# A four-layer graph network on one core: adj stored in the order of its reading, its small pieces loaded through GpSimd's queue, and a row added to x by GpSimd in four places

## The chip, the cores and the metric

The kernel is one program on one core of a Trainium2 chip. It is timed in device microseconds, and lower is better. The engines are named as the profile names them: PE (TensorE; PEld is its weight load), DVE (VectorE), ACT (ScalarE), POOL (GpSimd) and SP (SyncE, which only issues DMAs). All arrays are fp32.

## The reference

There are 16 graphs of 1024 nodes with 256 features. `adj` is 16 x 1024 x 1024, sparse, with a full diagonal. Four layers follow each other, each of the form `x = x + layer(relu(layernorm(x)), adj)`:

```python
# layer 0: attention; W_w, W_b, a_w
h = hidden @ W_w.T + W_b; u = mask * exp(e_i + f_j + a_b); h' = (u / sum(u)) @ h
# layer 1: normalised graph convolution; weight, bias
d = (sum(adj) + 1e-5) ** -0.5; out = d * (adj @ (d * (x @ weight))) + bias
# layer 2: 512-unit gates, node after node: node i reads what the nodes before it have become
x_par = norm_adjT[:, i] @ h; r, z = sigmoid(x W + x_par W'); h[i] = z * x_par + (1 - z) * tanh(...)
# layer 3: neighbour sum, two dense layers with an RMS norm between them
```

Only the order in which `adj` is stored for the device, the queue of some loads and the engine of two additions are at issue here. The values are the same.

## The kernel before

The program runs in three parts. `layers_0_1` takes the graphs one after the other in a software pipeline of 17 turns (`for i in range(B + 1)`). `layer_2` walks through 8 blocks of 128 nodes of all graphs. `layer_3` takes the graphs one by one again.

In `layers_0_1` every engine's order is the order in which the Python code runs (`tc.manual_schedule` holds PE, DVE, ACT, POOL and SP), so one late operand holds all that stands behind it on its engine. One turn i, in PE's order:

- `sums(i, ...)` for layer 0: seven products (L373) of quarters of the transposed adjacency with quarters of the features, in the manner of Strassen. Between the products stand hooks `a0` to `a6`, which hold work for the other engines.
- `weights` (L409 on PE, L412 on DVE: `x = po * scale + x`) for layer 0 of graph i and for layer 1 of graph i-1.
- `sums(i, ...)` for layer 1, with hooks `d0` to `d6`; then `degrees(i + 1)` (L450) for the next graph.

The operands of the products are the "quarters": 512 x 512 pieces of `adjT`, 1 MB each, held in ten buffers `at`. `get` (L289) loads five of them a graph; `plus` (L295) adds one to another with an accumulating DMA in POOL's queue; `drop` hands a buffer back. In hook `a0` of turn i, SP issues the load of x for graph i+1 and of three quarters (`b11`, `t1`, `b22`); `t3` and `b21` follow in `d0` and `d1`.

`plus_row` (L348) adds the row `W_b` to all of x after `degrees`, and the row `bias` in hook `d0`. It is an accumulating DMA of 1 MB in POOL's queue, once each a graph.

Beside this runs `orders`, a generator of small DVE steps which computes in what order layer 2 may take the nodes. `side(us)`, called in the hooks, lets so many microseconds of it run, counted by costs that are written beside each `yield`. Its input are the diagonal 128 x 128 blocks of `adj` in "pieces" `pc` of 4 rows. `fetch` (L102) loads a piece with eight DMAs of 32 KB in SP's queue, two pieces ahead of the one in use, into two buffers; `piece` (L107, DVE) waits for it. Each half of the generator, `places` and the chains in `rest`, reads 32 pieces, so there are 64 pieces and 512 DMAs. Between the halves, POOL loads four index tables (`table`, L182).

From turn 9 on, each turn also carries two "jobs" (`Job`), which prepare layer 2: `load` (ad, ab and h2 by SP), `mask` and `scale` (POOL, on ad and ab), `turn`, `first`, `order`, `base` (PE transposes and products, L522, L534, L546, L548), with stores by POOL.

In `layer_2`, `base_tasks.load` (L843) brings one column block `ab` of one graph's adj, 512 KB, 112 times; POOL masks it (L854) before PE uses it (L876).

The layer norms use `inv_sqrt`: a POOL power (L83, `rs` and `dis`) between two DVE instructions.

Of the kernel before, what the change touches and what calls it, by code (L numbers as in the profile page):

```python
# [16 lines left out]
P = 128  # L17
# [23 lines left out]
def gnn_stack(ctx: ExitStack, tc: tile.TileContext, a: dict, out: bass.AP):  # L41
# [51 lines left out]
    def orders(pool, psum):  # L93
# [3 lines left out]
        pieces = deque()  # L97

        def fetch(j0):
            nz = pool.tile([P, R, P], F32, name="pc", bufs=2)  # L100
            for t in range(NT):
                nc.sync.dma_start(nz[t * B : (t + 1) * B], a["adj"][:, t * P + j0 : t * P + j0 + R, t * P : (t + 1) * P])  # L102
            pieces.append(nz)

        def piece(j0, op, value):
# [12 lines left out]
        def places():  # L118
            nc.vector.memset(bins, TOP)
            nc.vector.tensor_scalar(open_, step[:, :S], -1.0, TOP - 1, op0=ALU.mult, op1=ALU.add)  # L120
            nc.vector.tensor_scalar(below, open_, 1.0, None, op0=ALU.add)
            nc.vector.memset(held, 0.0)
            fetch(0)
            fetch(R)
            yield 9.0
            for j0 in range(0, P, R):
                nz = piece(j0, ALU.is_equal, 2 * TOP)
                for j in range(j0, j0 + R):
                    mine = bins[:, j : j + 1]
# [12 lines left out]

            key = tile_("key")
            nc.vector.scalar_tensor_tensor(key, bins, -256.0, step, op0=ALU.mult, op1=ALU.add)
            for i in range(0, P, R):
                less = pool.tile([P, R, P], F32, name="pc", bufs=2)
                nc.vector.tensor_tensor(less, key[:, None].to_broadcast([P, R, P]),
                                        key[:, i : i + R][:, :, None].to_broadcast([P, R, P]), ALU.is_lt)
                nc.vector.tensor_reduce(pos[:, i : i + R], less, AX.X, ALU.add)
                yield 1.4  # L150
            pt = psum.tile([P, 512], F32, name="pt")
            nc.tensor.transpose(pt[:, :P], pos, ident)
            nc.vector.tensor_copy(place, pt[:, :P])
            yield 0.5
# [105 lines left out]
    def layers_0_1():  # L260
        with ExitStack() as st:
# [24 lines left out]

            def get(b, name, m, n):
                Q[b][name] = quarters.pop(0)
                nc.sync.dma_start(Q[b][name], rows(a["adjT"][b])[:, 4 * m : 4 * m + 4, 512 * n : 512 * n + 512])  # L289

            def drop(b, name):
                quarters.append(Q[b][name])
# [26 lines left out]
            class Moments:  # L319


                def __init__(self, x):
                    self.x = x
                    self.sum, self.ssq, self.neg = (small.tile([P, NT], F32, name=n) for n in ("m_sum", "m_ssq", "m_neg"))

                def first(self, tiles):
                    junk = psum.tile([P, 512], F32, name="pt")[:, :D]
# [16 lines left out]
                for t in tiles:  # L344
                    nc.scalar.activation(h[:, t], x[:, t], AF.Relu, bias=shift[:, t : t + 1], scale=scale[:, t : t + 1])

            def plus_row(x, name):
                nc.gpsimd.dma_start(out=x, in_=vec[name][:, None].to_broadcast([P, NT, D]), accum_op=ALU.add)  # L348

            def combos(h):  # L350

# [64 lines left out]
            def begin_f(b, tiles):  # L416
                m = mean[b]
                if tiles[0] == 0:
                    q[b] = big.tile([P, NT, D], F32, name="q")
                    m.f = small.tile([P, NT], F32, name="f")  # L420
                for t in tiles:
                    nc.scalar.activation(q[b][:, t], x[b][:, t], AF.Relu, bias=m.neg[:, t : t + 1])

# [7 lines left out]
            def end_f(b):  # L431
                m = mean[b]
                g[b] = gs
                nc.scalar.activation(g[b][:, :, 0], m.f, AF.Exp, bias=v[:, D : D + 1])
                m.rg = small.tile([P, NT], F32, name="rg")
                nc.vector.tensor_mul(m.rg, m.rs, g[b][:, :, 0])

            def scaled(b, tiles):
# [26 lines left out]
                return rc, deg  # L465

            def inverse(b, deg):
                zero = small.tile([P, NT], F32, name="zero")
                nc.vector.tensor_scalar(zero, deg, 0.0, None, op0=ALU.is_equal)
                safe = small.tile([P, NT], F32, name="safe")  # L470
                nc.vector.tensor_add(safe, deg, zero)
                nc.vector.reciprocal(safe, safe)
                nc.vector.tensor_scalar(zero, zero, -1.0, 1.0, op0=ALU.mult, op1=ALU.add)
                nc.vector.tensor_mul(dinv[:, b], safe, zero)

            class Job:
# [9 lines left out]
                def load(self):  # L486
                    b = self.b
                    self.ad = ad = self.tile("ad", [P, NT, 2 * P])
                    nc.sync.dma_start(ad[:, 0, P:], a["adjT"][b, :P, :P])
                    nc.sync.dma_start(ad[:, 1:], bass.AP(tensor=a["adjT"].tensor, offset=a["adjT"].offset + b * N * N + P * N,  # L490
                                                         ap=[[N, P], [P * N + P, NT - 1], [1, 2 * P]]))
                    self.ab = self.tile("ab", [P, NT, P])
                    nc.sync.dma_start(self.ab, rows(a["adj"][b])[:, :, :P])
                    if b < 14:
                        h2[b] = big.tile([P, NT, D], F32, name="h2", bufs=2)
                        nc.sync.dma_start(h2[b], rows(he_d[b]))
# [109 lines left out]
            add_halves(0, "t1", "t1", "b11")  # L606
            Q[0]["t2"] = quarters.pop(0)
            add_halves(0, "t2", "t1", "b22")
            plus_row(x[0], "W_b")
            left_of, first, second = combos(q[0])  # L610
            first()
            add_halves(0, "t3", "t3", "b22")
# [8 lines left out]
            for i in range(B + 1):  # L621
# [2 lines left out]
                got = {}  # L624

                def a0():
                    if ahead:
                        if i:
                            load_x(i + 1)
                        for name, mh, nh in (("b11", 0, 0), ("t1", 0, 1), ("b22", 1, 1)):  # L630
                            get(i + 1, name, mh, nh)
                    if run_a:
                        run_a.load()
                    side(1.0)
                def a1():
                    second()
                    add_halves(i, "t4", "t2", "b21")
                def a2_():
                    side(3.4)
                def a3():  # L640
                    side(2.6)
                def a4():
                    got["rc"], got["deg"] = over(i, ds)
                    if run_a:
                        run_a.mask()
                    if ahead:
                        mean[i + 1] = Moments(x[i + 1])
                        mean[i + 1].first(lo)
                    side(1.2)
# [72 lines left out]
                def d0():  # L722
                    if ahead:
                        plus(i + 1, "t1", "b11")
                        get(i + 1, "t3", 0, 1)
                    plus_row(x[i], "bias")
                    if m2:
                        m2.first(all_)
                    side(1.5)
                def d1():  # L730
                    second1()
                    if ahead:
                        get(i + 1, "b21", 1, 0)
                        begin_f(i + 1, all_)
                    side(0.6)
                def d2():
                    if m2:
                        m2.middle()
                        m2.second(all_)
                    if ahead:  # L740
                        add_f(i + 1, lo)
                    side(1.0)
                def d3():
                    if ahead:
                        add_f(i + 1, hi)
                        end_f(i + 1)
                    side(0.5)
# [21 lines left out]
                if ahead:  # L769
                    ds = degrees(i + 1)  # L770
                    plus(i + 1, "t3", "b22")
                    plus_row(x[i + 1], "W_b")
                    Q[i + 1]["t4"] = quarters.pop(0)
                if m2:
                    h2[i - 1] = big.tile([P, NT, D], F32, name="h2", bufs=2)
# [25 lines left out]
    def layer_2(shared, early):  # L801
        with ExitStack() as st:
# [33 lines left out]
            def base_tasks(t, bxt):  # L836
# [3 lines left out]

                def load(b):
                    ab = big.tile([P, NT, P], F32, name="ab")
                    nc.sync.dma_start(ab, rows(a["adj"][b])[:, :, t * P : (t + 1) * P])  # L843
                    hb = shared.tile([P, NT, D], F32, name="hb")
                    if t > 2:
                        nc.sync.dma_start(hb[:, : t - 2], rows(hn_d[b])[:, : t - 2])
# [797 lines left out]
```

## Time and profile before

| | |
|---|---|
| time, median of 3 runs | 4663.49 us (4662.62 to 4669.71) |
| profiled execution, its own time | 4668.5 us |
| profiled execution, span | 4666.8 us |
| granted TensorE clock, mean | 0.967 |
| PE busy | 4265.4 us (91%) |
| DVE busy | 2581.4 us (55%) |
| ACT busy | 1605.6 us (34%) |
| POOL busy | 1510.0 us (32%) |
| layers 0 and 1, 0 to 1540 us: PE, DVE, POOL busy | 1294.1, 930.2, 377.1 us |
| layer 2, 1540 to 3350 us: PE, DVE, POOL busy | 1685.5, 823.9, 570.9 us |
| layer 3, 3350 to 4667 us: PE, DVE, POOL busy | 1285.9, 827.2, 562.0 us |

Busy times of different engines overlap. "Idle before" an instruction is the time in which its engine had nothing to run, and the profile names what ended it. One product of four matmuls shows as eight records. The granted clock is the share of its full clock that TensorE was given in a stretch.

### The profile page before, as it was taken

The page shows a single profiled execution, that of the slowest core. Times are in us where ns is not written, and L with a number is a line of the kernel's source. Part 1 is how long each engine was busy: PE and PEld are TensorE (multiplying, and loading weights), DVE is VectorE, ACT ScalarE, POOL GpSimd, SP SyncE. Part 2 cuts the span into 40 slices and gives each one's busy share as a digit, 9 for nine tenths or more (in the row PEclk, how much of TensorE's full clock was granted, in tenths as well). Part 3 has the DMA queues.
Part 4 walks back from the last instruction along what each step waited for, and adds up shares of the span by engine and source line. Part 5 has one row for each costly group of instructions (what it writes and reads, how often), then busy time and mean ns, then how long its engine had stood idle before and what let it go on. Part 6 is the DMA issues. An engine that isn't in the chain of part 4 may idle for free. (4 is left out here: it accounts for less than half of the span.)

```text
span 4666.8 us, 56009 instructions
## 1 busy us (share of the span) xinstructions
PE 4265.4 (91%) x18967; PEld 2923.9 (63%) x18967; DVE 2581.4 (55%) x6213; ACT 1605.6 (34%) x3861; POOL 1510.0 (32%) x1720
## 2 busy tenths in 40 slices
PE   7898998777788799999999999999899999999998
PEld 3444454434445577878787878787655656565656
DVE  6676875455564344444444444445356767676765
ACT  2453554333342222322232322233333333333332
POOL 1111213321233332333222233333144353535352
PEclk9999999888899899999999999999899999999999
DMA  6576767866676644444544445442142323232310
GB/s 184 157 187 176 179 178 210 204 194 195 190 219 183 204 149 146 145 150 141 158 133 142 133 146 161 157 134 87 38 149 82 108 82 109 82 109 82 109 46 19
DMA packets 584232, 659.72 MB, mean 141 GB/s; under 512 B 49952, under 2 KB 480672, under 8 KB 577696
## 3 DMA queue, kind: packets, MB, share of 16 engines
q1 hardware_dynamic: 515168, 478.12, 32.4%
q0 software_dynamic: 68640, 176.45, 14.9%
q8 instruction: 204, 3.34, 0.3%
q14 instruction: 220, 1.80, 0.1%
HBM read 487.47 MB, written 116.65 MB: 129 GB/s over the span
## 5 line engine op out<-in xcount | busy, mean ns | idle before, releaser
L876 PE MATMUL pf<-hb,ab 128*128 128x256 f32 x1568 | 406.3, 381 | 15.5 <-DMA hb<-hs_d 6.2
L988 PE MATMUL pf<-hs,wx 128*128 128x256 f32 x1536 | 349.5, 382 | 22.8 <-POOL hs L979 21.1
L988 PEld LDWEIGHTS pf<-hs,wx 128*128 128x128 f32 x1536 | 290.9, 191 | 66.6 <-POOL hs L979 22.9
L83 POOL TENSOR_TENSOR rs<-rs_v,mhalf 128x8 f32<-128x8 f32 (+1 forms) x65 | 112.2, 1726 | 647.6 <-DVE rs_v L79 413.1
L876 PEld LDWEIGHTS pf<-hb,ab 128*128 128x128 f32 x1568 | 279.5, 190 | 67.5 <-issue 15.2
L1442 PE MATMUL ph<-bxt,hb 128*128 128x512 f32 x704 | 311.0, 598 | 4.7 <-ACT hb L1426 3.9
L409 PE MATMUL pmm<-w,ag 128*128 128x256 f32 x1024 | 253.9, 404 | 64.3 <-DVE ag L397 36.3
L1471 POOL TENSOR_TENSOR ss<-ss,sq 128x512 f32<-128x512 f32 x224 | 280.4, 1271 | 89.4 <-ACT sq L1469 85.6
L409 PEld LDWEIGHTS pmm<-w,ag 128*128 128x128 f32 x1024 | 201.9, 202 | 117.4 <-DVE x L412 40.1
L1532 PEld LDWEIGHTS po<-w,hh 128*128 128x128 f32 x2048 | 236.3, 193 | 9.5 <-issue 7.2
L1532 PE MATMUL po<-w,hh 128*128 128x128 f32 x2048 | 240.4, 277 | 1.4 <-ACT hh L1515 0.7
L1442 PEld LDWEIGHTS ph<-bxt,hb 128*128 128x128 f32 x704 | 133.2, 192 | 165.8 <-issue 160.1
L1276 POOL DMA_INDIRECT hs_d<-h,table x128 | 128.9, 1007 | 330.2 <-ACTq L1262 162.6
L993 DVE TENSOR_TENSOR gates<-pf,bias 128x512 f32<-128x512 f32 x128 | 88.2, 691 | 237.9 <-PE pf L988 230.4
L1514 DVE TENSOR_TENSOR hh<-hh,po 128x512 f32<-128x512 f32 x256 | 154.5, 680 | 96.7 <-PE po L1511 96.7
L1083 ACT ACTIVATE r<-pr 128x256 f32<-128x256 f32 (+3 forms) x230 | 68.0, 347 | 401.8 <-PE pr L1042 384.5
L1469 ACT ACTIVATE sq<-hh 128x512 f32<-128x512 f32 x224 | 141.2, 630 | 164.6 <-DVE hh L1467 126.1
L1024 PE MATMUL pf<-bd,h 128*128 128x384 f32 (+4 forms) x512 | 185.3, 453 | 4.6 <-ACT bs L863 2.8
L1467 DVE SCALAR_TENSOR_TENSOR hh<-ph,b,u 128x512 f32<-128x512 f32 x192 | 144.1, 751 | 65.3 <-PE ph L1463 55.1
L337 ACT ACTIVATE pt<-x,m_neg 128x256 f32<-128x256 f32 x240 | 114.3, 476 | 188.1 <-DVE m_neg L332 181.8
L1027 DVE TENSOR_TENSOR bxt<-bxt,pf 128x384 f32<-128x384 f32 (+4 forms) x256 | 124.9, 500 | 93.9 <-PE pf L1024 85.8
L1515 ACT ACTIVATE hh<-hh,rw 128x512 f32<-128x512 f32 x256 | 160.2, 710 | 15.7 <-DVE hh L1514 15.7
(350 smaller groups left out, 9165.9 us busy)
## 6 DMA issues: line engine op xcount, KB each, us to landing
at<-in_adjT SPq DMA_DIRECT2D x80, 1024.0 KB
ab<-in_adj SPq DMA_DIRECT2D x127, 512.0 KB
bxt<-in_adjT SPq DMA_DIRECT2D x88, 512.0 KB
at<-at POOLq DMA_DIRECT2D x30, 1024.0 KB, 7.5
at<-in_adjT SPq DMA_DIRECT2D x40, 512.0 KB
x<-W_b_sb POOLq DMA_DIRECT2D x16, 1024.0 KB, 14.7
pc<-in_adj SPq DMA_DIRECT2D x512, 32.0 KB
x<-bias_sb POOLq DMA_DIRECT2D x16, 1024.0 KB, 20.4
```

What stands on the lines that cost most here:

```text
L409: nc.tensor.matmul(po[:, t - t0], ag[:, c, t * P : (t + 1) * P], w[:, c], start=c == 0, stop=c == DC - 1)
L876: nc.tensor.matmul(pb, ab[:, jts[k]], hb[:, jts[k]], start=k == 0, stop=k == len(jts) - 1)
L988: nc.tensor.matmul(pg[:, e], wx[:, c, q * D + e * P : q * D + (e + 1) * P], self.hs[:, c], start=c == 0, stop=c == DC - 1)
L1024: nc.tensor.matmul(pf, h[:, g, c * P : (c + 1) * P], bd[:, g, b0 : b0 + n, S : S + far], start=True, stop=True)
L1276: nc.gpsimd.indirect_dma_start(out=hs_d[t][g][:, :], out_offset=row(1, g, t, s), in_=h[:, g], in_offset=None)
L1442: nc.tensor.matmul(pa, h[b][:, mt, c * P : (c + 1) * P], at[b][n0 // NH][:, mt], start=mt == 0, stop=mt == NT - 1)
L1467: nc.vector.scalar_tensor_tensor(hh[q][:, k], ph, b1[:, k : k + 1], u, op0=ALU.add, op1=ALU.add)
L1469: nc.scalar.activation(sq, hh[q][:, k], AF.Square)
L1471: nc.gpsimd.tensor_tensor(ss[q], ss[q], sq, ALU.add)
L1514: nc.vector.tensor_mul(hh[q][:, k], hh[q][:, k], pr)
L1515: nc.scalar.activation(hh[q][:, k], hh[q][:, k], AF.Silu, scale=rw[:, k : k + 1])
L1532: nc.tensor.matmul(po[:, n], left[:, c, n * P : (n + 1) * P], right[:, c], start=onto is None and n == 0 and c == 0, stop=c == HH - 1, ski ...
```

## The change

Four arrays are made on the host, each in the order in which the kernel reads it: `own` (the diagonal blocks, graph and block along the partitions), `quarters` (each 512 x 512 quarter with 8 KB together for each partition), `near` (the two blocks beside the diagonal that a job needs) and `columns` (each 1024 x 128 column block with 4 KB together for each partition). `adj` itself is no longer passed; `adjT` is, for layer 3.

- `fetch` becomes one DMA of 256 KB in POOL's queue, into three buffers instead of two. Six small tiles (`m_sum`, `f`, `rg`, `zero`, `safe`) go from two buffers to one.
- `get`, `Job.load` and `base_tasks.load` read the new arrays. The two loads of `ad` become one.
- `get` of `b11`, `t1` and `b22` moves from `a0` to `a1`, `a2_` and `a4`, so a job's first load comes ahead of them in SP's queue.
- `plus_row` becomes a POOL addition on two of the eight tiles of x. `W_b` is added after `degrees` and in `a0`, `a1` and `a2_`; `bias` in `d0` to `d3`.

```diff
         def fetch(j0):
-            nz = pool.tile([P, R, P], F32, name="pc", bufs=2)
-            for t in range(NT):
-                nc.sync.dma_start(nz[t * B : (t + 1) * B], a["adj"][:, t * P + j0 : t * P + j0 + R, t * P : (t + 1) * P])
+            nz = pool.tile([P, R, P], F32, name="pc", bufs=3)
+            nc.gpsimd.dma_start(nz, a["own"][:, j0 : j0 + R])
             pieces.append(nz)
...
             def get(b, name, m, n):
                 Q[b][name] = quarters.pop(0)
-                nc.sync.dma_start(Q[b][name], rows(a["adjT"][b])[:, 4 * m : 4 * m + 4, 512 * n : 512 * n + 512])
+                nc.sync.dma_start(Q[b][name], a["quarters"][b, m, n])
...
-            def plus_row(x, name):
-                nc.gpsimd.dma_start(out=x, in_=vec[name][:, None].to_broadcast([P, NT, D]), accum_op=ALU.add)
+            def plus_row(x, name, pair):
+                two = slice(2 * pair, 2 * pair + 2)
+                nc.gpsimd.tensor_tensor(x[:, two], x[:, two], vec[name][:, None].to_broadcast([P, 2, D]), ALU.add)
...
-                    nc.sync.dma_start(ad[:, 0, P:], a["adjT"][b, :P, :P])
-                    nc.sync.dma_start(ad[:, 1:], bass.AP(tensor=a["adjT"].tensor, offset=a["adjT"].offset + b * N * N + P * N,
-                                                         ap=[[N, P], [P * N + P, NT - 1], [1, 2 * P]]))
+                    nc.sync.dma_start(ad, a["near"][b])
                     self.ab = self.tile("ab", [P, NT, P])
-                    nc.sync.dma_start(self.ab, rows(a["adj"][b])[:, :, :P])
+                    nc.sync.dma_start(self.ab, a["columns"][b, 0])
...
                 def a0():
-                    if ahead:
-                        if i:
-                            load_x(i + 1)
-                        for name, mh, nh in (("b11", 0, 0), ("t1", 0, 1), ("b22", 1, 1)):
-                            get(i + 1, name, mh, nh)
+                    if ahead and i:
+                        load_x(i + 1)
                     if run_a:
                         run_a.load()
+                    if i:
+                        plus_row(x[i], "W_b", 1)
                     side(1.0)
                 def a1():
+                    if ahead:
+                        get(i + 1, "b11", 0, 0)
+                    if i:
+                        plus_row(x[i], "W_b", 2)
...
                 def a2_():
+                    if ahead:
+                        get(i + 1, "t1", 0, 1)
+                    if i:
+                        plus_row(x[i], "W_b", 3)
...
                 def a4():
+                    if ahead:
+                        get(i + 1, "b22", 1, 1)
...
                 def d0():
...
-                    plus_row(x[i], "bias")
+                    plus_row(x[i], "bias", 0)
...
                 if ahead:
                     ds = degrees(i + 1)
                     plus(i + 1, "t3", "b22")
-                    plus_row(x[i + 1], "W_b")
+                    plus_row(x[i + 1], "W_b", 0)
...
                 def load(b):
                     ab = big.tile([P, NT, P], F32, name="ab")
-                    nc.sync.dma_start(ab, rows(a["adj"][b])[:, :, t * P : (t + 1) * P])
+                    nc.sync.dma_start(ab, a["columns"][b, t])
```

`plus_row(x[i], "bias", k)` stands in `dk` for k = 1, 2, 3 as well, and before the first turn all four pairs of `W_b` are added to `x[0]` at once.

More of the change, by code (lines that the diff above doesn't have):

```diff
@@ L145, in places @@
             for i in range(0, P, R):
-                less = pool.tile([P, R, P], F32, name="pc", bufs=2)
+                less = pool.tile([P, R, P], F32, name="pc", bufs=3)
                 nc.vector.tensor_tensor(less, key[:, None].to_broadcast([P, R, P]),
@@ L323, in __init__ @@
                     self.x = x
-                    self.sum, self.ssq, self.neg = (small.tile([P, NT], F32, name=n) for n in ("m_sum", "m_ssq", "m_neg"))
+                    self.ssq, self.neg = (small.tile([P, NT], F32, name=n) for n in ("m_ssq", "m_neg"))
+                    self.sum = small.tile([P, NT], F32, name="m_sum", bufs=1)
                 def first(self, tiles):
@@ L419, in begin_f @@
                     q[b] = big.tile([P, NT, D], F32, name="q")
-                    m.f = small.tile([P, NT], F32, name="f")
+                    m.f = small.tile([P, NT], F32, name="f", bufs=1)
                 for t in tiles:
@@ L434, in end_f @@
                 nc.scalar.activation(g[b][:, :, 0], m.f, AF.Exp, bias=v[:, D : D + 1])
-                m.rg = small.tile([P, NT], F32, name="rg")
+                m.rg = small.tile([P, NT], F32, name="rg", bufs=1)
                 nc.vector.tensor_mul(m.rg, m.rs, g[b][:, :, 0])
@@ L467, in inverse @@
             def inverse(b, deg):
-                zero = small.tile([P, NT], F32, name="zero")
+                zero = small.tile([P, NT], F32, name="zero", bufs=1)
                 nc.vector.tensor_scalar(zero, deg, 0.0, None, op0=ALU.is_equal)
-                safe = small.tile([P, NT], F32, name="safe")
+                safe = small.tile([P, NT], F32, name="safe", bufs=1)
                 nc.vector.tensor_add(safe, deg, zero)
@@ L608, in layers_0_1 @@
             add_halves(0, "t2", "t1", "b22")
-            plus_row(x[0], "W_b")
+            for pair in range(4):
+                plus_row(x[0], "W_b", pair)
             left_of, first, second = combos(q[0])
@@ L730, in d1 @@
                 def d1():
+                    plus_row(x[i], "bias", 1)
                     second1()
@@ L736, in d2 @@
                 def d2():
+                    plus_row(x[i], "bias", 2)
                     if m2:
@@ L743, in d3 @@
                 def d3():
+                    plus_row(x[i], "bias", 3)
                     if ahead:
@@ L1606 @@
     adj = i["adj"]
+    adjT = adj.transpose(0, 2, 1)
+    tiles = adj.reshape(B, NT, P, NT, P)
+    near = np.zeros((B, P, NT, 2 * P), np.float32)
+    for t in range(NT):
+        lo = max(t - 1, 0) * P
+        near[:, :, t, 2 * P - ((t + 1) * P - lo) :] = adjT[:, t * P : (t + 1) * P, lo : (t + 1) * P]
     given = {
         "x": i["x"],
-        "adj": adj,
-        "adjT": adj.transpose(0, 2, 1),
+        "adjT": adjT,
+        "own": np.stack([tiles[:, t, :, t] for t in range(NT)]).reshape(NT * B, P, P),
+        "quarters": adjT.reshape(B, 2, 4, P, 2, 512).transpose(0, 1, 4, 3, 2, 5),
+        "near": near,
+        "columns": tiles.transpose(0, 3, 2, 1, 4),
         "W_w": i["L0_gnn_W_w"],
```

## The prediction

> **What bounds the kernel now.** I read the stretches first, one for each turn of the graph loop, cut where PE starts `degrees` (L450). Columns: us, then PE, PEld, DVE, ACT, POOL busy, granted clock, DMA share, GB/s.
>
> ```profile
> 415.80:496.60 80.80, 71.08 (x229) 36.52 (x230) 55.10 (x196) 36.35 (x105) 13.56 (x10) 0.96 0.65 168
> 496.60:564.60 68.00, 67.90 (x225) 35.77 (x224) 55.29 (x121) 36.35 (x105) 13.94 (x10) 1.00 0.72 186
> 638.30:707.00 68.70, 68.46 (x225) 35.70 (x224) 50.77 (x213) 36.34 (x105) 13.57 (x10) 1.00 0.71 184
> ...
> 1036.80:1175.00 138.20, 96.61 (x328) 53.13 (x328) 68.27 (x187) 41.76 (x115) 33.77 (x29) 0.83 0.66 189
> 1301.50:1395.80 94.30, 86.09 (x339) 50.00 (x338) 63.35 (x180) 41.77 (x115) 33.37 (x29) 1.00 0.78 231
> ```
>
> The same work takes PE 68 us without idle time in two turns, and 77 to 81 us in the five turns before them. With two jobs it takes 94.3 us in the last row and 126.4, 138.2 and 126.5 us in the three turns ahead of it. PE is the bound where a turn is short; elsewhere something holds PE, and its clock drops as well. The waits of 0 to 1540 us name it, PE's and then DVE's (us in total, times, longest):
>
> ```profile
> PE pz L373 <- DVE ag L393: 69.3, 7, 16.5
> PE pmm L409 <- DVE ag L397: 36.3, 6, 7.7
> PE pmm L409 <- DVE x L412: 24.5, 9, 8.6
> ```
>
> ```profile
> DVE pc L107 <- DMA pc<-in_adj: 155.2, 21, 17.1
> ```
>
> PE waits for DVE, which has nothing wrong with it but that it stands at a piece. The timelines of PE, DVE and SP show one such place:
>
> ```profile
> 973.79 6.59 PE L373 MATMUL pz<-at,q 128*128 128x512 f32 x8 [15.38 <-DVE ag L393]
> ```
>
> ```profile
> 967.82 0.38 DVE L107 TENSOR_SCALAR pc<-pc 128x416 f32<-128x416 f32 x1 [15.48 <-DMA pc<-in_adj]
> ...
> 973.05 0.68 DVE L393 TENSOR_TENSOR ag<-pz,ag 128x512 f32<-128x512 f32 x1
> ```
>
> ```profile
> 910.58 33.89 SPq L102 DMA_DIRECT2D pc<-in_adj  x24
> 944.64 0.38 SPq L274 DMA_DIRECT2D x<-in_x  x1
> 945.14 2.50 SPq L289 DMA_DIRECT2D at<-in_adjT  x3
> 947.74 1.65 SPq L489 DMA_DIRECT2D ad<-in_adjT  x1
> ```
>
> The pieces for 967 us stand in SP's queue behind the loads of x, three quarters and a job, issued from 944.6 to 958.2 us, and SP itself was held at older pieces until 944.5. The order of one queue is the bound here, not a busy engine. After 1540 us little is to be had: layer 2 keeps PE busy 1685.5 of 1810 us, and of 3350 to 4667 us 1285.9 of 1317; the chain of waits there is matmul after matmul. The chain doesn't reach back before 3205 us, so I don't use it for the loop.
>
> **The pieces (fetch).** 512 SP DMAs go, 64 POOL DMAs of the shape of L295 come (0.94 us each, 60 us of POOL in all). The third buffer matters: a piece is fetched two ahead into a buffer that DVE left one group earlier, so POOL rarely waits and runs ahead of DVE. A group of four columns in `places` takes DVE some 5 us (48.4 to 55.6 us, with other work), in `rest` 3 us (930.5 to 933.5). The lead is thus 6 us or more against 0.94 us of issue and a landing of 3 to 5 us (3.3 for `aj`, 4.9 for `x_d` by the page).
> Value: the five turns at 77.3, 81.2, 80.2, 80.5 and 80.8 us sum to 400.0; at 68.35 each, the mean of the two clean turns, 341.8: -58.2. The three job turns sum to 391.1. Their model is the turn of 94.3 us, which reads no piece, less 2.5 us of a PE wait that only it has (`o_open`, L232): 91.8 each, 275.4: -115.7. Cross-check from the waits: L393 and L397 give 105.6 us, 12.0 us more stand before `px` at "issue" just after piece waits, and PE's busy time shrinks by some 41 us as its clock comes back (about 3.3 in each of five turns, 8 in each of three). That is 159 against 174.
> The Trainium skill speaks against this edit ("DMA: Bandwidth & Descriptors", "Issuing engines are not separate DMA queues"): all queues run on the same 16 DMA engines, and issuing from another engine saves only the issuing time. By that rule the sum is about 0, since SP's issue time bounds nothing. The SP rows decide: what a piece waits for is the loads ahead of it in its own ring and SP's stalls, and the clean turns ran at a DMA share of 0.71 to 0.78, higher than the slow turns' 0.66. I take the row.
> What is left: pieces now stand behind POOL's other DMAs and waits. At a turn's end L295 waits for PE (104.5 us in 15), then `he_d`, in job turns `near_d`, `next_d` and `base_d` (landing 8 to 11 us), go ahead of a piece. DVE came to its third piece after such a stretch at 942 us, with that piece behind `base_d` of 931 us in the new order, so it may just miss. I put 2.5 us on each job turn and 0.5 on each of five others: +10. Bounds: 0, and 6 us in each of the eight, 48.
>
> **The row additions (plus_row).** 32 DMA issues go (30.2 and 27.7 us of POOL), 128 POOL additions of 128x512 come. The same form is L1430, 1272 ns: 163 us. With the pieces, POOL rises from 377 to about 542 us over the loop; it is not full. All wait for operands long ready, and the users are far off (`W_b` is added by the third product, L412 reads it after the seventh). But POOL's power `rs` and DVE's reads stand beside them. L605 takes 1218 ns alone and up to 2145 beside POOL, L765 156 ns and up to 1519:
>
> ```profile
> L605 DVE TENSOR_TENSOR at<-at,at x68: 1216/1218/2145, 22.9 to 1418.1; 128x1024 f32<-128x1024 f32 x68
> L765 DVE TENSOR_TENSOR m_shift<-m_neg,rs x15: 156/156/1519, 174.7 to 1482.1; 128x8 f32<-128x8 f32 x15
> ```
>
> The Trainium skill ("SBUF — State Buffer", "Who interferes with whom") says that a DVE instruction with two SBUF inputs and a POOL instruction that reads SBUF exclude each other for the whole instruction. By the rule eight additions a turn could cost DVE 8 x 1.27 = 10 us, 163 in all. By the rows a collision costs 0.9 to 1.4 us, only some of DVE's instructions pay, and DVE has 12 us free in a 68 us turn. I take 1 us a turn on the path: +16, with bounds of 0 and 80. In return 32 MB of accumulating DMA leave POOL's queue (14.7 and 20.4 us to landing), which is what lets a piece behind `he_d` land in time; that is already in the piece value.
>
> **The moved loads.** A job's `ad` and `h2` come ahead of three quarters. At 733 us POOL waited 8.5 us for `ad`, DVE 8.2 us for POOL's iota behind it, PE 6.8 us: -7. At 853 us PE waited 7.3 us for `h2`; but in that turn POOL's four table loads hold `dis` until 861.9 us and DVE's `rd` until 870.0, so PE would wait there instead: 0, or +5 with the adds and two piece issues in POOL's order. Quarters issued one to four hooks later are read a turn later; their cover is the rest of a 68 us turn, and the waits for them (L450, 16.5 us, partly in the job turns) rather shrink: -3.
>
> **The other layouts.** Quarters, near blocks and columns move the same bytes in fewer packets. No row shows such packets in SP's queue. If they are slower, L450 waits longer, if faster its 16.5 us go: bounds of +10 and -16, and I keep the -3 above, the nearest row being the quarters' own, which nearly always come in time today. In layer 2 POOL idles 267.7 us for `ab`, but PE waits for POOL only 21.1 us, all before 1575 us, for `he`. I take -5, with bounds of +10 and -25.
>
> **Sum.** -58.2 - 115.7 + 10 + 16 - 7 - 3 - 5 = -162.9. From the profiled execution's 4668.5 us that is 4505.6. The median of the runs lies 5.0 us under that execution: about 4500.
>
> **Rivals.**
> Half of it: DVE, at 63 to 72 us busy in a job turn, and POOL, at 33 plus some 13, come too close to PE, and the job turns end at 110 us. That gives -61 for -116: 4555. For it: in-order engines with three busy partners; against it: the 94.3 us turn had DVE at 63.4.
> The pieces were late for want of bandwidth, and a new queue brings them no earlier. Then only the lighter traffic counts, perhaps 30 us: 4633. Against it: the DMA shares above.
> More: no residue, and layer 2 gains: 4500 - 26 - 20, about 4455.
> Slower: at the end of a turn POOL's head stands at L295, `he_d` or a power, the piece behind it is late, and DVE stops as before. The place is L107. It decides from the average wait for a piece: now 155.2 / 64 = 2.4 us; with the same path to PE the gain is eaten at (155 + 163) / 64 = 5.0 us for each of the 64. One landing behind a stalled head (up to 24.7 us at L295) is as long, but it would have to be every second piece: 4700.
> That the change doesn't do what it says I leave out: in the built order each piece is one POOL DMA, and 128 additions stand where the 32 DMAs were.
>
> **The numbers.** Forecast 0.67, half 0.17, more 0.06, bandwidth 0.05, slower 0.05. My own case spans 4465 to 4535 by the bounds of its terms. With the half case and part of the larger gain, 4450 to 4585 holds 8 in 10. A difference under 0.2% (9 us) can't be told from none. Faster 0.94, same 0.01, slower 0.05.
>
> **What would show it.** Right: the wait of L107 under 30 us; turns 1 to 5 at 68 to 71 us with a clock near 1.00; job turns 11 to 13 at 90 to 97; L349 with 128 additions of about 1.3 us; layer 2 within 10 us of 1810. Wrong: L107 still above 80 us, now behind POOL; DVE idle for POOL's `rs` well over 18 us; L605 or L198 longer throughout.

## The result: faster by 1.6%, under half of what was forecast

Median of four runs 4588.1 us (4584.4 to 4591.9), against 4663.1 us (4658.1 to 4669.7) for the kernel before in the same session: ratio 0.9838, 95% interval 0.9821 to 0.9856. The forecast was 4500 us with a range up to 4585. The gain is 75 us where 163 were expected.

The same five turns as before, by the same columns (us, PE, PEld, DVE, ACT, POOL busy, granted clock, DMA share, GB/s), now read:

```profile
409.30:488.00 78.70, 72.17 (x225) 36.72 (x224) 63.97 (x196) 36.46 (x105) 21.98 (x19) 0.96 0.44 144
488.00:559.30 71.30, 68.47 (x225) 35.67 (x224) 63.62 (x121) 36.45 (x105) 20.70 (x16) 1.00 0.46 148
637.40:708.80 71.40, 68.77 (x229) 35.69 (x230) 58.51 (x213) 36.50 (x105) 20.34 (x16) 1.00 0.46 148
1004.80:1113.20 108.40, 89.97 (x327) 50.44 (x326) 81.18 (x187) 41.85 (x115) 46.19 (x45) 0.94 0.61 210
1215.30:1314.50 99.20, 88.42 (x342) 51.11 (x342) 67.47 (x180) 41.77 (x115) 40.26 (x35) 0.97 0.59 203
```

Read them in pairs with the rows before. The slow turn of the first half went from 80.8 to 78.7 us only. The two clean turns, 68.0 and 68.7 us before, became *longer*, 71.3 and 71.4. The job turn fell from 138.2 to 108.4, and the turn that was its model rose from 94.3 to 99.2. DVE's column is the new thing: it is 8 to 13 us higher in the first four rows and 4 in the last, though DVE has not one instruction more; POOL's rose by 7 to 12. The DMA share of the first three rows fell from between 0.65 and 0.72 to about 0.45.

The waits of 0 to 1500 us, PE's and DVE's (us, times, longest):

```profile
DVE pc L106 <- DMA pc<-in_own: 28.9, 8, 6.5
PE pz L374 <- DVE ag L394: 19.9, 11, 4.6
PE pmm L410 <- DVE x L413: 17.4, 6, 12.0
PE px L374 <- DVE o_fit L129: 13.0, 5, 3.5
PE px L374 <- DVE s L359: 7.0, 3, 2.3
```

The wait for pieces fell from 155.2 to 28.9 us, as forecast, and PE's longest wait for L394 from 16.5 to 4.6 us. But two lines are new: PE waits for DVE's `o_fit` in each of turns 1 to 5 and for `s` in turns 6 to 8, where no piece is late. (In both lines PE's product reads `s`; `o_fit` is the DVE instruction that ended just before PE went on.) The timeline of one clean turn shows such a place (start, length, engine, line, what it wrote and read, idle before it):

```profile
534.69 5.26 POOL L349 TENSOR_TENSOR x<-x,bias_sb 128x512 f32<-128x512 f32 x4
535.35 5.17 DVE L358 TENSOR_TENSOR s<-h 128x512 f32<-128x512 f32 x1 [2.53 <-ACT h L345]
540.55 0.69 DVE L359 TENSOR_TENSOR s<-s,h 128x512 f32<-128x512 f32 x1
541.39 1.96 PE L374 MATMUL px<-at,s 128*128 128x512 f32 x4 [2.33 <-DVE s L359]
```

L358 is a subtraction of 0.68 us. Here it takes 5.17 us: it ends half a microsecond after the last of POOL's four additions. L359, free of POOL, takes 0.69 us, and PE, which wanted `s` 2.3 us earlier, waits. Over the whole run:

```profile
L349 POOL TENSOR_TENSOR x<-x,W_b_sb x64: 1255/1278/2333, 22.0 to 1331.3; 128x512 f32<-128x512 f32 x64
L604 DVE TENSOR_TENSOR at<-at,at x68: 1209/1217/2300, 23.3 to 1335.3; 128x1024 f32<-128x1024 f32 x68
L358 DVE TENSOR_TENSOR s<-h x16: 679/1525/6562, 72.3 to 1375.1; 128x512 f32<-128x512 f32 x16
L129 DVE SCALAR_TENSOR_TENSOR o_fit<-o_below,o_bins,o_open x128: 221/233/6010, 47.4 to 469.8; 128x16 f32<-128x16 f32 x128
L384 DVE TENSOR_TENSOR ag<-ag,py x32: 666/680/689, 35.0 to 1381.6; 128x512 f32<-128x512 f32 x32
L208 DVE TENSOR_REDUCE o_top<-o_junk x8: 285/286/288, 1228.5 to 1235.6; 128x1 f32<-128x128 f32 x8
```

Columns of durations are min/median/max in ns. DVE instructions with two inputs in SBUF are stretched: L604 to nearly twice its length, L358 to almost ten times, L129 to 26 times. An addition with one input in PSUM (L384) keeps its length, though 9 of the 32 stood beside a POOL addition, and so does the reduction L208 with its one input, of which 3 of 8 did. One input in SBUF is not always safe, however. L106, which scales a piece in place, takes 0.17 to 0.42 us for 61 of the 64 pieces of the run h1 below, but twice it stood beside a row of four additions and took 5.6 us. One of the two:

```profile
1057.70 5.62 DVE L106 TENSOR_SCALAR pc<-pc 128x192 f32<-128x192 f32 x1
1057.92 5.28 POOL L349 TENSOR_TENSOR x<-x,bias_sb 128x512 f32<-128x512 f32 x4
```

Where the 80 us between the two profiled spans (4666.8 and 4586.7) came from, by sums of turns:

| stretch | before | forecast | after |
|---|---|---|---|
| turns 1 to 5 | 400.0 | 349.3 | 391.9 |
| turns 6 to 8 | 210.5 | 213.5 | 220.7 |
| turns 9, 10 | 203.4 | 198.4 | 189.0 |
| turns 11 to 13 | 391.1 | 285.9 | 317.5 |
| turns 14, 15 | 236.9 | 238.9 | 241.6 |
| after turn 15 | 3128.5 | 3123.5 | 3129.8 |

The 3 us for the quarters and the 1 us for the rows of turn 0 are in no row of the forecast's column.

### The profile page after: what moved, and what is told of

It reads as the page before. It is cut to its first block, busy times and chain, and to the rows that moved or that the text cites. A ratio compares the mean times of both kernels' runs of the same rounds, so it can differ in the third digit from the quotient of the medians.

```text
span 4586.7 us, 55389 instructions
## 1 busy us (share of the span) xinstructions
PE 4255.1 (93%) x18967; PEld 2921.0 (64%) x18967; DVE 2718.0 (59%) x6213; ACT 1606.4 (35%) x3861; POOL 1653.1 (36%) x1880
## 5 line engine op out<-in xcount | busy, mean ns | idle before, releaser
L888 PE MATMUL pf<-hb,ab 128*128 128x256 f32 x1568 | 407.9, 383 | 16.5 <-DMA hb<-hs_d 7.2
L410 PE MATMUL pmm<-w,ag 128*128 128x256 f32 x1024 | 242.2, 393 | 33.7 <-DVE x L413 17.4
L410 PEld LDWEIGHTS pmm<-w,ag 128*128 128x128 f32 x1024 | 196.9, 196 | 80.8 <-DVE x L413 29.8
L1112 DVE TENSOR_TENSOR w<-w,hc 128x256 f32<-128x256 f32 (+3 forms) x230 | 87.4, 380 | 138.8 <-ACT hc L1111 138.7
```

The lines of the kernel that those rows point to most:

```text
L410: nc.tensor.matmul(po[:, t - t0], ag[:, c, t * P : (t + 1) * P], w[:, c], start=c == 0, stop=c == DC - 1)
L888: nc.tensor.matmul(pb, ab[:, jts[k]], hb[:, jts[k]], start=k == 0, stop=k == len(jts) - 1)
```

## The experiments

The theory after this reading: POOL's additions lock DVE out for their whole length, and that ate the gain. The rival: the pieces in POOL's queue are worth less than forecast. Ratios are against the kernel before, run in the same session (its medians there were 4667 to 4671 us). Turn sums are cut as above.

**e1_rows_by_dma: the changed kernel, with the rows added by DMA again.**

```diff
-                nc.gpsimd.tensor_tensor(x[:, two], x[:, two], vec[name][:, None].to_broadcast([P, 2, D]), ALU.add)
+                nc.gpsimd.dma_start(out=x, in_=vec[name][:, None].to_broadcast([P, NT, D]), accum_op=ALU.add)
```

The calls stand in the two old places again.

> The changed kernel with one part undone: the rows are added again by one accumulating DMA each, in the two old places. Theory (POOL's additions lock DVE out: 8 of them, 10 us in all, lengthen DVE's work by 8 to 11 us a turn): DVE busy per turn falls back to about 55 us in turns 1 to 8, turns 1 to 5 take 69 to 71 us at a clock near 1.00 instead of 78 to 79, turns 6 to 8 some 3 us less, job turns 11 to 13 about 97 instead of 106; total 4505 to 4535. Rival (the pieces behind POOL's other work are what eats the gain): the two accumulating DMAs stand ahead of pieces in that queue, the waits of DVE for pieces grow from 29 us, total 4580 to 4620.

Measured: 4548.0 us (4547.4 to 4548.5), ratio 0.9741 (0.9725 to 0.9758). L358 (here L357) never takes more than 0.69 us, and DVE's busy time per turn is back at 50.8 to 57.7 us in turns 1 to 8 and turns 6 to 8 are back at 210.2, so the lockout is real and worth 40 us net. But turns 2 to 5 still take 72.6 to 76.8 us, turns 11 to 13 sum to 317.8, as in the changed kernel, and DVE waits for pieces twice as long as there:

```profile
DVE pc L106 <- DMA pc<-in_own: 63.1, 10, 13.6
```

The time lies between both expectations: neither theory is the whole.

**e2_rows_only: the kernel before, with only the additions by POOL** (the diff of e1 the other way round, on the old kernel).

> The kernel before with only the additions of the rows moved to POOL's 128 instructions, in the changed kernel's places; pieces, loads and layouts as before. Theory (lockout): DVE busy over the loop grows by 130 to 160 us; where DVE waits for pieces a part of it is hidden, so the time grows by 20 to 70 us, to 4685 to 4730. Rival (the lighter DMA traffic pays for it): 4630 to 4660.

Measured: 4649.0 us (4642.1 to 4652.7), ratio 0.9957 (0.9943 to 0.9971): 20 us *faster*; the rival was right. Turns 6 to 8 pay (210.5 to 221.1), but the wait for pieces in SP's queue falls from 155.2 to 94.0 us. 32 MB of accumulating DMA are gone; that this is the reason was not shown apart. The same edit gains 20 us where pieces are late and costs 40 where they mostly are not.

**e3_pieces_only: the kernel before, with only the pieces changed.**

```diff
-            nz = pool.tile([P, R, P], F32, name="pc", bufs=2)
-            for t in range(NT):
-                nc.sync.dma_start(nz[t * B : (t + 1) * B], a["adj"][:, t * P + j0 : t * P + j0 + R, t * P : (t + 1) * P])
+            nz = pool.tile([P, R, P], F32, name="pc", bufs=3)
+            nc.gpsimd.dma_start(nz, a["own"][:, j0 : j0 + R])
```

> The kernel before with only the pieces changed: one DMA each from the new layout, in POOL's queue, three buffers (and the six small tiles at one buffer). Rows by DMA, loads and layouts as before. Theory: this part alone is worth more than the whole change, 130 to 165 us: 4500 to 4535, with turns 1 to 5 at 69 to 71 us. Rival (the pieces' part was over-valued, and the turns have another limit at 78 us): 4580 to 4600.

Measured: 4564.0 us (4561.5 to 4566.5), ratio 0.9774 (0.9757 to 0.9790). This part alone is worth 104 us, more than the whole change, but well short of 130 to 165. DVE still waits 51.3 us for pieces.

**e4_layouts_only: the kernel before, with `quarters`, `near` and `columns` read from the new arrays**, loads in their old places.

> The kernel before with only the layouts of quarters, near blocks and columns changed; pieces, row additions and the places of the loads as before. Theory: nothing waits for these bytes except behind the pieces: 4650 to 4665. Rival (shorter landings also bring the pieces earlier, since they stand behind quarters in SP's queue): 4610 to 4640, with DVE's wait for pieces well under 155 us.

Measured: 4650.5 us (4645.5 to 4653.7), ratio 0.9958 (0.9941 to 0.9975): at the edge of the theory, a small real gain of 18 us, nearly all in turns 9 to 13 (594.5 to 573.4), with the wait for pieces hardly changed (148.2 us).

Alone on the old kernel, the three parts gain 20, 104 and 18 us; all together, with the moved loads, they gain 75. The moved loads were in no run alone. e1 differs from e3 by them and the layouts, and is 16 us faster, about what the layouts give.

**g1_rows_by_dve: the changed kernel, with the 128 additions on DVE itself.**

```diff
-                nc.gpsimd.tensor_tensor(x[:, two], x[:, two], vec[name][:, None].to_broadcast([P, 2, D]), ALU.add)
+                nc.vector.tensor_tensor(x[:, two], x[:, two], vec[name][:, None].to_broadcast([P, 2, D]), ALU.add)
```

> The changed kernel with all 128 additions of the rows on DVE instead of POOL, in the same places. Theory (a POOL addition of 1.28 us locks DVE out for about its whole length, so DVE loses 8 to 11 us a turn by work that it does not do): on DVE an addition of 128x512 takes 0.68 us, 8 of them 5.5 us a turn, so DVE's busy time per turn falls by 2 to 5 us against the changed kernel, DVE's pair of sums s (L358, L359, now 2.6 and 1.35 us in the mean) goes back to 0.68 us each, and the time falls to 4555 to 4580. Rival (POOL's additions run beside DVE for the most part): DVE's busy time rises by 5 us a turn against the changed kernel, 4610 to 4640.

Measured: 4546.9 us (4538.4 to 4558.1), ratio 0.9742 (0.9717 to 0.9768), 41 us under the changed kernel and 8 us below even the theory's range. An addition takes 684 ns on DVE (median of 128), and DVE's busy time in turns 1 to 8 is 3 to 7 us *lower* than when POOL does the work:

```profile
L358 DVE TENSOR_TENSOR s<-h x16: 681/692/693, 73.3 to 1332.0; 128x512 f32<-128x512 f32 x16
```

The same L358 as above, with POOL's additions out of the way: never over 693 ns. This is the cleanest proof of the lockout: taking on all the work costs DVE less than standing beside it.

**g2_pieces_act_queue: e1, with the pieces issued in ACT's queue.**

```diff
-            nc.gpsimd.dma_start(nz, a["own"][:, j0 : j0 + R])
+            nc.scalar.dma_start(nz, a["own"][:, j0 : j0 + R])
```

> Rows by accumulating DMA as in e1_rows_by_dma, and the pieces in ACT's queue instead of POOL's. It tells what makes the last piece of each burst late. Theory A (the 16 DMA engines are full there, whatever the queue): waits of DVE for pieces within 20 us of the 63 of e1_rows_by_dma, total 4540 to 4560. Theory B (the order in POOL's queue, behind the accumulating DMAs and the stores): the waits fall under 25 us, job turns 11 to 13 to 95 to 100 us, total 4500 to 4525.

Measured: 4508.6 us (4500.1 to 4509.8), ratio 0.9655 (0.9639 to 0.9672). Theory B, and by 40 us. DVE's wait for pieces is down to 9.6 us:

```profile
DVE pc L106 <- DMA pc<-in_own: 9.6, 5, 3.9
```

The windows of a turn of the first half, a clean one and a job turn of this kernel (the columns as above) are what the prediction had promised for the changed kernel:

```profile
371.90:441.30 69.40, 68.78 (x228) 35.66 (x228) 54.89 (x196) 36.35 (x105) 13.56 (x10) 1.00 0.71 193
441.30:509.30 68.00, 67.90 (x225) 35.79 (x224) 55.29 (x121) 36.36 (x105) 13.94 (x10) 1.00 0.69 186
943.20:1038.40 95.20, 86.44 (x327) 49.80 (x329) 68.06 (x187) 41.85 (x115) 33.50 (x29) 0.98 0.84 260
```

So the pieces' value was right, and POOL's queue did not deliver it. The timeline of e1 at the start of a turn shows why (POOL's issues and DVE's piece):

```profile
245.16 0.95 POOL L294 DMA_DIRECT2D at<-at  x1 [6.26 <-PE pt L450]
245.78 1.96 POOL L348 DMA_DIRECT2D x<-W_b_sb  x1
250.57 0.93 POOL L778 DMA_DIRECT2D he_d<-h  x1 [2.83 <-ACT h L345]
251.49 1.14 POOL L101 DMA_DIRECT2D pc<-in_own  x2
...
265.68 0.28 DVE L106 TENSOR_SCALAR pc<-pc 128x240 f32<-128x240 f32 x1 [5.34 <-DMA pc<-in_own]
```

And in g2 the loads of the same piece (240 columns wide when DVE uses it) and of the next two, with the places where DVE uses the first two of them:

```profile
237.54 0.34 ACTq L101 DMA_DIRECT2D pc<-in_own  x1
248.06 4.41 ACTq L101 DMA_DIRECT2D pc<-in_own  x2
```

```profile
252.01 0.28 DVE L106 TENSOR_SCALAR pc<-pc 128x240 f32<-128x240 f32 x1
257.61 0.27 DVE L106 TENSOR_SCALAR pc<-pc 128x224 f32<-128x224 f32 x1
```

In e1 POOL stands 6.3 us at L294 and 2.8 at `he_d` before it may issue the two pieces, and then they lie in its queue behind three transfers of 1 MB. The packet records of that queue keep this order: 128 packets of 8 KB (the quarter's addition) from 246 to 252 us, then 1024 of 1 KB (`W_b`) to 261, then those of 4 KB (`he_d` and the pieces); DVE has its piece 14 us after the issue. In ACT's queue the packets of the piece issued at 237.5 us run from 239.2 to 245.1, side by side with the quarter's addition in POOL's queue and ahead of all of `W_b`. Those of the next two run from 252.9 to 258.4 us, when the engines are as full as in e1. DVE doesn't wait.

POOL's queue is not slow for its own sake. In e1 a piece issued at 198.9 us, with nothing ahead of it, and one issued at 222.4 us, behind three transfers of 1 MB, took to landing (last column, us):

```profile
pc<-in_own POOLq DMA_DIRECT2D x1, 256.0 KB, 2.9
```

```profile
pc<-in_own POOLq DMA_DIRECT2D x1, 256.0 KB, 19.3
```

**g3_wb_later: e1, with `W_b`'s DMA issued after hook `a2_`** of the same turn, behind the burst's pieces.

```diff
                     side(3.4)
+                    if i:
+                        plus_row(x[i], "W_b")
...
-                    plus_row(x[i + 1], "W_b")
```

> e1_rows_by_dma with the accumulating DMA of W_b for graphs 1 to 15 issued after hook a2_ instead of at the end of the turn before, so that it stands behind the pieces of that burst and not ahead of them. If the waits for pieces come from what stands ahead of them (queue or full DMA engines, 2 MB of traffic less ahead of them): they fall from 63 us to 20 to 40, total 4515 to 4540. If x is now late for DVE's L412 (it is read some 15 us later): PE waits there 2 to 5 us a turn, total 4560 to 4600.

Measured: 4540.0 us (4536.0 to 4546.2), ratio 0.9719 (0.9701 to 0.9737); waits for pieces 50.2 us. At the edge of the first expectation for the time, outside it for the waits; 8 us under e1. One transfer fewer ahead of the pieces is not enough.

**g4_no_rows: e1 without any addition of rows** (left out of the computation).

```diff
-            plus_row(x[0], "W_b")
...
-                    plus_row(x[i], "bias")
...
-                    plus_row(x[i + 1], "W_b")
```

> e1_rows_by_dma with the additions of the rows W_b and bias left out of the computation altogether, so the time is that of the rest. It gives the price of the rows by POOL (the changed kernel less this one) and by DMA (e1_rows_by_dma less this one). Theory (rows cost DVE its time by POOL, and the pieces theirs by DMA): 4500 to 4525, waits for pieces under 30 us; rows by POOL then cost 65 to 85 us where I had put 16, by DMA 25 to 45. Rival (job turns and turns 1 to 5 have another limit than pieces and rows): 4535 to 4550, with turns 11 to 13 still at 102 to 108 us.

Measured: 4534.1 us (4532.1 to 4545.5), ratio 0.9716 (0.9695 to 0.9738), waits for pieces still 49.7 us, turns 11 to 13 at 303.3. The rival's number, within 1 us; its turns 11 to 13 take 97.8 to 103.9 us where it had 102 to 108. Rows cost 54 us by POOL (4588.1 - 4534.1), 14 by DMA and 13 by DVE. Without rows there is still something to find.

**h1_after_act_queue: the changed kernel with the one-word edit of g2.**

> The changed kernel with one word different: the pieces are issued in ACT's queue instead of POOL's; rows by POOL. Theory (the piece's queue and the rows' lockout are two separate losses): 4540 to 4555, 35 to 48 us under the changed kernel, with turns 11 to 13 at 96 to 101 us but turns 1 to 5 still at 74 to 78, since DVE is stretched there. Rival (the lockout alone holds the changed kernel, the pieces cost it nothing now, as its waits of 28.9 us suggest): 4575 to 4590.

Measured: 4557.7 us (4553.0 to 4566.2), ratio 0.9759 (0.9742 to 0.9775): 30 us under the changed kernel, 3 us outside the theory, far from the rival. Turns 1 to 5 take 74.6 to 75.9 us and turns 11 to 13 sum to 302.8 (317.5). The changed kernel's wait of 28.9 us understated what the queue cost; a likely reason is that DVE, stretched by POOL, came to the pieces later.

**h2_dve_rows_act_queue: both repairs** (the edits of g1 and g2 on the changed kernel).

> The changed kernel with both repairs: rows added by DVE, pieces in ACT's queue. Theory: no lockout, 32 MB of accumulating DMA less, 5.5 us a turn more on DVE, which is at 61 of 69 us: 4495 to 4512, turns 1 to 5 at 69 to 71 us, turn 10 at about 101 where g2_pieces_act_queue had 110. Rival (DVE, now busier and still in order, holds PE as in the changed kernel): 4520 to 4545.

Measured: 4513.6 us (4510.9 to 4519.6), ratio 0.9672 (0.9656 to 0.9688), 2 us over the theory. Turns 1 to 5 at 70.0 to 71.7 us. As good as g2 within what a session tells apart.

**h3_no_rows_act_queue: g4 with the edit of g2** (rows left out).

> Pieces in ACT's queue, and the additions of the rows W_b and bias left out of the computation altogether, so the time is the floor under the changed kernel with pieces that come in time and rows that cost nothing. Theory: 4480 to 4500 (my sum without its row term and its residue is 4474). Rival (something else holds turns 1 to 5 and 11 to 13): over 4505.

Measured: 4492.6 us (4489.7 to 4497.4), ratio 0.9624 (0.9607 to 0.9640): the theory. Turns 1 to 5 sum to 345.9 us (the prediction's model said 341.8), turns 11 to 13 to 287.5 (275.4), turns 6 to 8 to 210.6. No third large cost is left.

**h4_pieces_sp_queue: e3, but the pieces stay in SP's queue.**

```diff
-            nc.gpsimd.dma_start(nz, a["own"][:, j0 : j0 + R])
+            nc.sync.dma_start(nz, a["own"][:, j0 : j0 + R])
```

> The kernel before with the pieces in the new layout, one DMA of 256 KB each and three buffers, but still in SP's queue, behind the loads of x and the quarters. Theory (the order of that queue was the bound, not the eight small DMAs): 4630 to 4660, with waits of DVE for pieces over 100 us. Rival (the layout and the single DMA are what helps): 4560 to 4580, as with e3_pieces_only.

Measured: 4604.1 us (4600.6 to 4611.4), ratio 0.9859 (0.9842 to 0.9875), between the two: waits of 102.3 us, as the theory has it, but 63 us are gained in the queue that I had called the bound. One DMA in place of eight, with a third buffer (the two were not tried apart), is worth 63; POOL's queue adds 40 (e3).

**i2_he_act_queue: e1, with the store `he_d` in ACT's queue**, pieces still in POOL's.

```diff
-                    nc.gpsimd.dma_start(rows(he_d[i - 1]), h2[i - 1])
+                    nc.scalar.dma_start(rows(he_d[i - 1]), h2[i - 1])
```

> Rows by DMA and pieces in POOL's queue as in e1_rows_by_dma; only the store he_d, 1 MB a turn, which stands ahead of two pieces at a turn's end, is issued in ACT's queue. The bytes are the same. If the pieces are late for what stands ahead of them in POOL's queue: waits for pieces fall from 63 us to 30 to 45, total 4520 to 4538. If they are late because POOL's kind of queue or the full DMA engines are slow whatever the order: 4543 to 4553.

Measured: 4543.0 us (4541.8 to 4549.8), ratio 0.9725 (0.9710 to 0.9739); waits 48.1 us. The time is the second expectation's, on its edge, and the waits lie just over the first's. The trace decides more than the time: in the turn shown above, counted from the turn's start, POOL now issues the first piece 4.9 us earlier (at 245.9 us), and DVE uses it 1.7 us earlier (at 263.3). Its packets again wait for the quarter's addition and `W_b` to pass, 1 KB packets until 261 us. So it is mainly what is ahead in the queue, not when POOL gets to the issue. Counted from the turn's start, g2 issues this piece only 1 us earlier than i2, at 3.7 against 4.7 us. In g2 its packets are through 7.6 us after the issue; in i2 it lands 17.3 us after it. Most of what is ahead is the two accumulating transfers. A run with all three gone from the burst was not made.

**i3_mixed: g2, with the rows of graphs 9 and 10 by DVE.**

```diff
+                if b in (9, 10):
+                    nc.vector.tensor_tensor(x[b][:, two], x[b][:, two], vec[name][:, None].to_broadcast([P, 2, D]), ALU.add)
+                elif pair == 0:
+                    nc.gpsimd.dma_start(out=x[b], in_=vec[name][:, None].to_broadcast([P, NT, D]), accum_op=ALU.add)
```

> g2_pieces_act_queue (pieces in ACT's queue, rows by DMA), but with the rows of graphs 9 and 10 by DVE, since turns 9 and 10 took 184.7 us in h2_dve_rows_act_queue against 193.2 us here, and all other turns were shorter with DMA. Expected: 4498 to 4506, the lowest of all; if turn 10's gain came from DMA traffic of other graphs, 4506 to 4512.

Measured: 4504.0 us (4497.1 to 4505.4), ratio 0.9642 (0.9628 to 0.9655). Turns 9 and 10 sum to 186.3 us, against 193.2 in g2: the accumulating DMAs of these two graphs held turn 10. It has the lowest median of the kernels that compute everything; against g2 the intervals overlap, so only the turns tell them apart.

Medians side by side, in us:

| rows \ pieces in | POOL's queue | ACT's queue |
|---|---|---|
| by POOL | 4588.1 (the changed kernel) | 4557.7 |
| by DMA | 4548.0 | 4508.6 |
| by DVE | 4546.9 | 4513.6 |
| left out | 4534.1 | 4492.6 |

Down a column is the price of the rows, across a row that of the queue: 30 to 42 us whichever way the rows are added. Rows by POOL cost 54 us in the first column and 65 in the second. The two costs nearly add. Medians of different sessions are good to some 5 us.

## Why the prediction was wrong

The bound was read rightly: pieces held DVE, DVE held PE. Three terms of the sum, 4500 = 4474 + 16 + 10, went wrong. The first comes back to the collisions of DVE with POOL in the kernel before, of which these lines show one:

```profile
1033.69 1.89 POOL L511 TENSOR_TENSOR ad<-ad,dinv 128x1024 f32<-128x1024 f32 x1
1034.09 1.52 DVE L765 TENSOR_TENSOR m_shift<-m_neg,rs 128x8 f32<-128x8 f32 x1
```

- **The row additions: 16 forecast, 54 measured** (by POOL less left out). This is the step that failed most. I weighed the Trainium skill ("SBUF — State Buffer", "Who interferes with whom": a POOL instruction that reads SBUF and a DVE instruction with two SBUF inputs exclude each other for the whole instruction) against rows in which a collision cost 0.9 to 1.4 us, and took the rows. But those rows did not speak against the rule. What collided there was not POOL's power, which the prediction names, but the jobs' masks and scalings, and the delay was about what was left of POOL's instruction when DVE's began. In the lines above L765, 0.16 us long when alone, ends at 1035.61, 0.03 us after L511; all seven stretched L765 of that run end so, 0.02 to 0.03 us after a scaling. The rows were the rule at work, on few instructions. In the changed kernel the eight additions of a turn keep POOL busy for 10.5 to 11.3 us in turns 1 to 8, and DVE paid 7.7 to 11.6 us (its busy time against e1): about the rule in full. "DVE has 12 us free" was an average again: the free time stood elsewhere, and `s`, which PE needs next, was among what was stretched.
- **The residue: 10 forecast, 41 measured** (g4 less h3). I had listed what would stand ahead of a piece in POOL's queue, L295, `he_d` and the stores, and priced it at 2.5 us in three turns. It is the old fault in a new queue: a late piece in each of turns 2 to 5 and 11 to 13, behind megabytes. The landing of 3 to 5 us was too short as well: in the changed kernel a piece took 6.7 us in the median and up to 16.0. The bound of 48 would have held it. That the accumulating rows' leaving "lets a piece behind `he_d` land in time" was wrong: without any rows the waits were still 49.7 us.
- **The rest: 4474 forecast, 4492.6 measured** (h3). Turns 1 to 5 and 6 to 8 were right within some 4 us; turns 11 to 13 are 12 us longer than the model, turns 9 and 10 are 10 us shorter, and the 8 us put on the quarters and layer 2 did not come: everything after turn 15 takes 3129.8 us in the changed kernel, 3128.5 before.

The misses sum to 38 + 31 + 19 = 88 us, the whole difference, as they must by the way they are taken. Taken in the other order (h1 less h3, changed kernel less h1), the rows cost 65 us and the residue 30, so either step failed by a factor of three or more. Both bounds (80 and 48) held their own term, but the range reached the case of one of them being high, not of both.

The queue rule of the Trainium skill that I had set aside ("DMA: Bandwidth & Descriptors", "Issuing engines are not separate DMA queues": issuing elsewhere saves only issue time) was wrong here, as I had said, and for more than I had said. With one layout and three buffers, the kernel takes 4604.1 us with the pieces in SP's queue and 4564.0 in POOL's; with rows by DMA and all the new layouts, 4548.0 in POOL's and 4508.6 in ACT's. The queues share the engines, but not what stands ahead of a piece. It was not only that order, though: h4 gained 63 us in SP's own queue, and how much of that is the single DMA and how much the third buffer stays open.

Of the rivals, "half" at 4555 came nearest, and for a related reason: DVE was filled, but by the lockout rather than by its own work.

## What to carry to other kernels

Before work moves to POOL, count the DVE instructions with two SBUF inputs that run beside it, and those that scale in place like L106, and charge POOL's whole length to DVE; if DVE can do the work in about half that length, as here (0.68 for 1.28 us), leave it on DVE. A small, urgent transfer belongs in a queue without large ones ahead of it: ask of the new queue what you asked of the old. Two edits that each help alone can spoil each other, so measure the parts on top of each other, not only one by one on the old kernel.

## What was not expected of the hardware

- The lockout can last over a whole row of POOL additions: a DVE subtraction of 0.68 us took 5.17 us beside four of them, and up to 6.56 us in the run. It need not: in h1, beside three additions from 181.85 us on, L129, L131 and L132 each got in after one of them, at 1.28, 0.97 and 1.18 us. A PSUM input kept L384 at 666 to 689 ns, but one SBUF input did not keep L106 from 5.6 us.
- Transfers in POOL's queue went through in the order of issue, seen in the sizes of their packets. The row's accumulation of 1 MB in packets of 1 KB took some 9 us in e1. From 252 to 260 us that queue took 88% of the 16 engines' time, and all queues together moved only 206 GB/s.
- Small PE gaps cost twice. In the changed kernel, gaps of 2.6 us before 203.2 us and of 2.2 us before 233.5 us were each followed by some 3.4 us at a granted clock of 0.50 (windows 203.0 to 206.4 and 233.7 to 237.1). Its turns 1 to 5, with 5.6 to 7.2 us of gaps, ran at a mean of 0.956 to 0.957, and PE was busy for 71.5 to 72.5 us in them, against 68.4 to 68.8 us in turns 2 to 5 of g2; its turns 6 and 8, with 2.8 us of gaps or less, kept 1.00. The sum of the gaps does not decide: turn 4 of e2 had 7.8 us of them, none over 2.3 us, and kept 1.00; turn 5 of g3 had 3.6 us, nearly all in one gap, and ran at 0.954.
